# Layer 2's rows as 128 and twice 64 channels, its values kept in DRAM per pixel

## The chip, the cores and the metric

The program runs on one core of a Trainium2 chip. The core has a matrix engine (TensorE, PE in the profile), three engines for element-wise work (VectorE or DVE, ScalarE or ACT, GpSimd or POOL), a queue engine that issues most of the transfers (SyncE or SP), and 16 DMA engines. Each engine runs its own instructions in order; they wait for each other on semaphores. The metric is the device time of one execution in microseconds (us), lower is better. Three runs of the kernel before gave a median of 6404.84 us (6400.07 to 6409.53).

## The reference

Four layers follow each other on four images of 192 channels and 64 by 64 pixels in float32. The change lies in the third, "layer 2", an attention over overlapping windows of 8 by 8 pixels that stand 6 pixels apart, after three pixels of padding on each side (11 by 11 windows):

```python
DIM, HEADS, WS, OVERLAP, PAD = 192, 6, 8, 2, 3
STRIDE = WS - OVERLAP
...
y = _conv1x1(_ln_c(x, n1g, n1b), qkv_w, qkv_b)      # norm over channels, then 192 -> 576
cols = _unfold(y, WS, STRIDE, PAD)                  # zero padding comes after the projection
win = cols.reshape(B, 3 * HEADS, ch, WS * WS, L).transpose(0, 4, 1, 3, 2)
q = win[:, :, :HEADS] * temp[None, None]
k = win[:, :, HEADS:2 * HEADS]
v = win[:, :, 2 * HEADS:]
attn = jnp.einsum('blhic,blhjc->blhij', q, k) + bias[None, None]
e = jnp.exp(attn - jnp.max(attn, axis=-1, keepdims=True))
s_img = _reverse(jnp.sum(e, axis=-1, keepdims=True), H, W)      # sums folded back to pixels
o_img = _reverse(jnp.einsum('blhij,blhjc->blhic', e, v), H, W)  # outputs folded back to pixels
out = (o_img / s_img[:, :, None]).reshape(B, C, H, W)
```

What follows in layer 2 (a projection, a gate and an MLP) and the other layers (a deformable attention, a non-local block, a masked convolution) are not touched.

## The kernel before

For each image the kernel runs layer 1, then `windows()` (line 1060), the windowed attention, then the rest of layer 2 with layer 3. The image lies in DRAM (`x_flat`, of which `x_drams` is a view as two halves of 96 channels); `windows()` leaves its result in `oi` in SBUF. Constants are made early, in `constants()` (line 186), one step at a time beside the gather of the first image; there the weights of the three projections, `qkvT`, are loaded as two halves of 96 rows with a row of biases below the second, and the norm's gain, its offset and its mean are folded into them.

`windows()` goes over 11 rows of windows (`wr`). Of each row of windows only the pixel rows that are new are normed and projected; two pixel rows are shared with the row of windows before and copied by POOL (`shared`, line 1131). For one row of windows the parts are:

- `load` (1077): one transfer of the new pixel rows, 96 partitions of twice 384 pixels, into `xr`.
- `norm_steps` (1107): squares on ACT, sums over channels on PE, the inverse root on DVE and ACT, spread by PE, and two DVE products into `xs`, a padded strip of pixel rows.
- `project_rows` (1142): for each half of the channels a product for queries and one for keys, 384 columns wide, each with a first part of 96 rows (L1150) and a second of 97 (L1151, the biases included); ACT empties each into `qs` (L1154) and `ks` (L1156).
- `queries` and `inputs` (1168, 1172): POOL copies `qs` and `xs` window by window into `qw` and `xw` (L1163 to L1165).
- `scores` (1176): products of 32 rows per window and head on PE, then bias, maximum and subtraction on DVE. `exponentials` (1201): ACT, then sums on DVE.
- `turned` (1216): for each pair of windows the values are projected from `xw` (L1225) and copied by ACT (L1230); the exponentials are transposed by PE (L1233) and copied by ACT into `et` (L1237).
- `outputs` (1243): the products of values and exponentials (L1253), which fold windows into pixels in PSUM as they accumulate. `collect` (1266) copies them out, `finish` (1295) divides.

A row's 11 windows are taken in three groups of four (`g`), each group in two pairs. Products wait for a PSUM slot where they share one: the tag "a" has two slots, for the projections, the values, the transposes and the spread sums alike.

The order on each engine is written out by hand (`tc.manual_schedule()`, line 1308): what stands earlier in the loop is issued earlier on its engine. In a step of a group the next group's scores come first; then for each pair the transposes and values of this pair, the outputs of the pair before, and beside them work for later rows: in `g == 0` the projections of row `wr + 1`, one half of the channels after each pair; in `g == 1` a load and the sums of the norm of row `wr + 2`; in `g == 2` the rest of that norm, and the division for row `wr - 1`:

```python
for pair in range(WG // 2):
    ops = turned(wr, g, pair, ex)
    if due is not None:
        outputs(*due)
        ...
    due = ops
    if g == 0 and wr + 1 < NWIN:
        project_rows(wr + 1, pair)
```

SP takes its transfers in the same order. In this stage those are the loads of `xr` and, after the second row of windows, `load_image` (2022), 16 transfers of the whole image for the part that follows, with two by two partitions of 128 and 64.

Of the kernel before, what the change touches and what calls it, by code (L numbers as in the profile page):

```python
# [69 lines left out]
_WIDE = ["l0_bfc2", "l2_projb", "l2_hftw", "l2_hftb", "l2_fc2b", "l3_bias", "l3_b2"]  # L70
# [11 lines left out]
def conv_seq_kernel(ctx: ExitStack, tc: tile.TileContext, a, out: bass.AP):  # L82
# [86 lines left out]
    for i in range(3):  # L169
# [4 lines left out]
        thetaT, phiT, gT, wW, qkvT, bias, v48, headsel, fc1_dram, fc1_bias, fc1b_dram, fc1b_bias, outb,  # L174
    ) = (None for _ in range(13))
# [10 lines left out]
    def constants():  # L186

        nonlocal thetaT, phiT, gT, wW, qkvT, bias, v48, headsel, fc1_dram, fc1_bias, fc1b_dram, fc1b_bias, outb
# [13 lines left out]
        qkvT = const([P + 1, 2, 3 * C], "qkvT")  # L202
        in_turn(nc.sync.dma_start(out=qkvT[:P], in_=a["qkvT"].rearrange("(k p) n -> p k n", p=P)))
        in_turn(nc.sync.dma_start(out=qkvT[P : P + 1, 1, :], in_=a["qkvb"]))
# [56 lines left out]
        with pool_of(name="foldq", bufs=1, space=PSUM) as pp:  # L261
            p = pp.tile([128, 2, 512], F32, tag="p", name="p_qkv")
            n = 3 * C // 2
            for u in range(2):
                for k in range(2):
                    nc.tensor.matmul(
                        p[P : P + 1, u, 0:n], lhsT=V["l2_n1b"][:, k], rhs=qkvT[:P, k, bass.ts(u, n)], start=k == 0, stop=k == 1
                    )
            row = qkvT[P : P + 1, 1, :].rearrange("p (u n) -> p u n", u=2)
            nc.vector.tensor_tensor(row, row, p[P : P + 1, :, 0:n], ALU.add)  # L270
            for k in range(2):
                nc.vector.tensor_scalar_mul(qkvT[:P, k, :], qkvT[:P, k, :], V["l2_n1g"][:, k])
            centred(qkvT[:P], pp)
# [72 lines left out]
    x_flat = [dram.tile([C, HW], F32, tag=f"xd{i}", name=f"xd{i}") for i in range(2)]  # L346
    xn_drams, x_drams = ([t.rearrange("(k p) n -> p k n", p=P) for t in ts] for ts in (xn_flat, x_flat))
# [712 lines left out]
    def windows(b, oi, load_image):  # L1060
# [3 lines left out]
        with ExitStack() as s:  # L1064
# [4 lines left out]
            given, norms, xws, qws = {}, {}, {}, {}  # L1069

            def new_rows(wr):

                top = STRIDE * wr - PAD
                r0, r1 = (PAD if wr == 0 else WS - STRIDE), min(WS, H - top)
                return r0, r1, top + r0

            def load(wr, by=nc.sync):
                r0, r1, at = new_rows(wr)
                t = given[wr] = sb.tile([P, 2, 512], F32, tag="xr", name=f"xr_{b}_{wr}")[:, :, 0 : (r1 - r0) * W]
                by.dma_start(out=t, in_=x_drams[b % 2][:, :, at * W : (at + r1 - r0) * W])  # L1080
# [6 lines left out]
            for j in range(2):  # L1087
                xs = s1.tile([P + 1, 2, WS, SW], F32, tag=f"xs{j}", name=f"xs{j}_{b}")
                qs = s1.tile([P, 2, WS, SW], F32, tag=f"qs{j}", name=f"qs{j}_{b}")
                ks = s1.tile([P, 2, WS, SW], F32, tag=f"ks{j}", name=f"ks{j}_{b}")  # L1090
                for t in (xs, qs, ks):
                    nc.gpsimd.memset(t, 0.0)

                nc.gpsimd.memset(xs[P : P + 1, 1, (PAD if j == 0 else 0) : WS, inside], 1.0)
                sets.append((xs, qs, ks))
            ets = []
            for j in range(3):
                et = s1.tile([128, 3, 2, WS, WS + STRIDE], F32, tag=f"et{j}", name=f"et{j}_{b}")
                nc.gpsimd.memset(et, 0.0)
                ets.append(et)  # L1100
            rss = []
# [5 lines left out]
            def norm_steps(wr, src, dst, rows):  # L1107

                n, name = src.shape[2], f"l2n1_{b}_{wr}"
                q = n // 4  # L1110
                sq = s1.tile([P, 2, 512], F32, tag="ln_sq", name=f"sq_{name}", bufs=2)[:, :, :n]
                nc.scalar.activation(sq, src, AF.Square)
                yield SQUARE
                pv = ps.tile([128, 512], F32, tag="n", name=f"pv_{name}")
                variances(pv[:, 0:q], src, mean192)
                variances(pv[:, 128 : 128 + q], sq, mean192)
                r = s1.tile([128, 128], F32, tag="ln_r", name=f"r_{name}", bufs=2)[:, 0:q]
                spread_variance(r, pv[:, 0:q], pv[:, 128 : 128 + q])
                yield from inverse_root_steps(r, r)
                pb = spread_quarters(r, n, P, ps, name).rearrange("p (r c) -> p r c", r=rows)  # L1120
                for k in range(2):
                    nc.vector.tensor_tensor(dst[:, k], src[:, k, :].rearrange("p (r c) -> p r c", r=rows), pb, ALU.mult)

            def norm(wr, upto=None):

                r0, r1, _ = new_rows(wr)
                if wr not in norms:
                    norms[wr] = norm_steps(wr, given.pop(wr), sets[wr % 2][0][:P, :, r0:r1, inside], r1 - r0)
                links(norms[wr], upto)

            def shared(wr, i):

                to, of = sets[wr % 2][i], sets[1 - wr % 2][i]
                r1 = new_rows(wr)[1]
                if i == 0 and wr == 2:
                    nc.gpsimd.memset(to[P : P + 1, 1, PAD - 1 : PAD, inside], 1.0)
                if wr > 0:
                    nc.gpsimd.tensor_copy(to[:, :, 0 : WS - STRIDE, :], of[:, :, STRIDE:WS, :])
                if r1 < WS:
                    nc.gpsimd.memset(to[:, :, r1:WS, :], 0.0)  # L1140

            def project_rows(wr, h):

                xs, qs, ks = sets[wr % 2]
                r0, r1, _ = new_rows(wr)
# [964 lines left out]
```

## Time and profile before

| what | us |
|---|---|
| median of three runs | 6404.84 |
| the profiled execution | 6392.29 |
| its span, first to last instruction | 6390.5 |
| windows stage of the first image, from the square of its first norm at 1480.17 to the outputs' last copies at 1744 | 264 |
| pitch of two rows of windows in the middle of that stage | 23.04 |

In the stretch from 1480 to 1747 us PE is busy for 244.96 us, DVE for 160.52, ACT for 166.93 and POOL for 76.94, and the mean granted clock of PE is 0.98. The stage runs four times, once an image. The copies of finished rows (L1271) start at 1526.91, 1549.21, 1572.29, 1595.33, 1618.39, 1641.43, 1664.48, 1687.52, 1710.50, 1730.70 and 1744.02, which gives the length of each row: the first and the last ones are shorter, for they have less to do for other rows.

A line of a group reads: line of the code, engine, operation, what is written and read, then the number of instructions and their times. PE is the matrix product, PEld its loading of weights. A float32 product appears as two instructions. Where a time is followed by a bracket, that is how long the engine sat idle before, and who ended the wait.

### The profile page before, as it was taken

Reading aid. Unit: us, or ns where it says so; the run is one execution under the profiler, and the core shown is the slowest. Engines: PE = TensorE matmul, PEld = TensorE weight load, DVE = VectorE, ACT = ScalarE, POOL = GpSimd, SP = SyncE. Lnnn points to the kernel's source line nnn. Section 1 sums busy time; section 2 is a strip of 40 time slices with the busy share of each in tenths; the row PEclk is TensorE's granted clock in tenths of the full one; section 3 lists DMA queues with packets and bytes.
Section 4 is the critical chain, followed back from the end, with each engine's and each line's share of the span. In section 5 each row is a group of like instructions: output and inputs, shape, how many; then the busy total and the mean of one; then the engine's idle time right before and its main releaser. Section 6 shows DMA issues by size and latency. Waiting matters only on the chain.

```text
span 6390.5 us, 106371 instructions
## 1 busy us (share of the span) xinstructions
PE 5900.9 (92%) x40528; PEld 4039.0 (63%) x40528; DVE 4612.9 (72%) x6850; ACT 3779.2 (59%) x6552; POOL 2111.3 (33%) x2293
## 2 busy tenths in 40 slices
PE   7888999999989899999988899999998989999897
PEld 4455588886544568887654458888654457776543
DVE  3864199985677669996676839998567867765667
ACT  3764388875654358885654438887565536545542
POOL 2763077752200047772210017775220000003200
PEclk8989999999989999999999999999998999999998
DMA  6995267751010267772110057775111010001000
GB/s 193 308 316 152 81 195 223 224 178 37 24 29 17 74 200 221 226 222 69 35 36 24 21 145 227 222 223 171 36 27 29 21 57 11 13 15 38 5 7 22
DMA packets 330117, 698.60 MB, mean 109 GB/s; under 512 B 59894, under 2 KB 216838, under 8 KB 328839
## 3 DMA queue, kind: packets, MB, share of 16 engines
q0 software_dynamic: 92736, 455.22, 22.0%
q1 hardware_dynamic: 236038, 235.78, 13.5%
q8 instruction: 321, 5.26, 0.3%
q14 instruction: 190, 1.55, 0.1%
q10 hardware_dynamic: 832, 0.79, 0.0%
HBM read 611.25 MB, written 78.87 MB: 108 GB/s over the span
## 4 chain that ended last, share of the span: by engine, by line
PE 63%; DVE 20%; ACT 5%; DMA 5%; issue 4%; SPq 2%; POOL 1%; POOLq 0%; DVEq 0%; ACTq 0%
PE y L1041 11%; PE s L973 10%; PE h L650 7%; DVE ha L1403 2%; PE h L1595 2%; PE qk L1150 2%; PE v L1225 2%; PE o L878 2%; PE qk L1151 2%; DMA ring<-table,idx 2%; DVE ga L1403 2%; PE po L538 2%; DVE gate L1403 2%; DVE row L639 1%; DVE top L980 1%
## 5 line engine op out<-in xcount | busy, mean ns | idle before, releaser
L632 POOL DMA_INDIRECT ring<-table,idx x1152 | 1671.1, 1451 | 946.0 <-DVE row L639 172.7
L973 PE MATMUL s<-ths,ph 96*128 96x256 f32 x4096 | 982.5, 381 | 6.4 <-ACT sc L975 4.0
L973 PEld LDWEIGHTS s<-ths,ph 96*128 96x128 f32 x4096 | 776.6, 191 | 131.1 <-ACT sc L975 6.3
L638 ACT ACTIVATE row<-ring,pos 128x384 f32<-128x384 f32 x1152 | 673.0, 609 | 240.4 <-DVE xo L643 147.2
L639 DVE SCALAR_TENSOR_TENSOR row<-ring,fr,row 128x384 f32<-128x384 f32 x1152 | 673.1, 611 | 111.2 <-ACT row L638 106.3
L1041 PE MATMUL y<-sc,gx 128*97 128x256 f32 x3008 | 716.4, 379 | 0.0
L1041 PEld LDWEIGHTS y<-sc,gx 128*97 128x97 f32 x3008 | 489.3, 164 | 127.5 <-issue 5.1
L642 ACT ACTIVATE xo<-row,pos 128x192 f32<-128x192 f32 x1152 | 485.5, 448 | 64.2 <-PE h L650 32.2
L643 DVE SCALAR_TENSOR_TENSOR xo<-row,fr,xo 128x192 f32<-128x192 f32 x1152 | 445.4, 411 | 41.5 <-ACT xo L642 39.3
L975 ACT COPY sc<-s 128x1024 f32<-128x1024 f32 x376 | 377.1, 1003 | 157.0 <-PE s L973 154.2
L1038 DVE TENSOR_TENSOR sc<-sc,mbs 128x1024 f32<-128x1024 f32 x376 | 453.0, 1217 | 19.8 <-ACT mbs L999 19.7
L1039 ACT ACTIVATE sc<-sc 128x1024 f32<-128x1024 f32 x376 | 393.3, 1053 | 75.2 <-DVE sc L1038 72.1
L980 DVE TENSOR_TENSOR top<-top,sc 128x1024 f32<-128x1024 f32 x282 | 344.0, 1220 | 128.6 <-ACT sc L975 128.4
L650 PE MATMUL h<-ti,xo 128*128 128x192 f32 x2304 | 434.6, 327 | 0.0
L650 PEld LDWEIGHTS h<-ti,xo 128*128 128x128 f32 x2304 | 388.8, 190 | 28.8 <-issue 8.2
L1205 DVE TENSOR_REDUCE eh<-ex 128x12 f32<-128x768 f32 x132 | 125.4, 950 | 317.1 <-ACT ex L1203 317.1
L1403 DVE SCALAR_TENSOR_TENSOR ga<-gate,v,ga 128x1024 f32<-128x1024 f32 x234 | 300.3, 1283 | 6.7
L650 PE MATMUL h<-kept,xo 128*128 128x192 f32 x960 | 239.2, 381 | 70.5 <-DVE xo L643 62.0
L1645 POOL COPY gate<-gate 128x192 f32<-128x192 f32 x12 | 4.2, 348 | 904.9 <-ACT gate L1638 904.9
L650 PEld LDWEIGHTS h<-kept,xo 128*128 128x128 f32 x960 | 169.7, 210 | 162.9 <-DVE xo L643 116.4
L855 PE MATMUL h<-d_l0m,fc 128*128 128x256 f32 x768 | 217.5, 427 | 59.1 <-ACT z L1601 22.5
L1041 PE MATMUL y<-se,gx 128*97 128x256 f32 x1088 | 261.1, 380 | 0.5 <-ACT yn L1047 0.5
(402 smaller groups left out, 11090.8 us busy)
## 6 DMA issues: line engine op xcount, KB each, us to landing
ti<-table SPq DMA_DIRECT2D x768, 48.0 KB
ring<-table,idx POOLq DMA_INDIRECT x1152
xnd<-xn SPq DMA_DIRECT2D x4, 3270.0 KB
xi<-in_x_dram SPq DMA_DIRECT2D x32, 384.0 KB
xk<-xd SPq DMA_DIRECT2D x32, 384.0 KB
xd<-xc SPq DMA_DIRECT2D x64, 192.0 KB
table<-tt SPq DMA_DIRECT2D x32, 384.0 KB
xc<-xd SPq DMA_DIRECT2D x60, 192.0 KB
```

Of the source, the lines that this page charges most:

```text
L632: nc.gpsimd.indirect_dma_start(out=gt.rearrange("p q r c -> p (q r c)"), out_offset=None, in_=corners, in_offset=bass.IndirectOffsetOnAxis ...
L638: nc.scalar.activation(row, gt[:, 0], AF.Copy, scale=pos[:, t, 9 + tap : 10 + tap])
L639: nc.vector.scalar_tensor_tensor(row, gt[:, 1], fr[:, t, 9 + tap : 10 + tap], row, ALU.mult, ALU.add)
L642: nc.scalar.activation(xo[:, j, :], row[:, 0, :], AF.Copy, scale=pos[:, t, tap : tap + 1])
L643: nc.vector.scalar_tensor_tensor(xo[:, j, :], row[:, 1, :], fr[:, t, tap : tap + 1], xo[:, j, :], ALU.mult, ALU.add)
L650: nc.tensor.matmul(acc[m // 2][:, bass.ts(m % 2, C)], lhsT=xo.rearrange("p j c -> p (j c)")[:, bass.ts(m, 128)], rhs=tt, start=t == 0 and ...
L973: nc.tensor.matmul(p[:, t, :], lhsT=ph[:, bass.ts(G * g + t, 128)], rhs=ths[i], start=True, stop=True)
L980: nc.vector.tensor_tensor(tops[i], tops[i], to, ALU.max)
L1038: nc.vector.tensor_tensor(ex, ex, mbs[i].unsqueeze(1).to_broadcast([128, G, QN]), ALU.add)
L1039: nc.scalar.activation(ex, ex, AF.Exp)
L1041: nc.tensor.matmul(py, lhsT=gx[:, G * g + t, :], rhs=ex[:, t, :], start=g == 0 and t == 0, stop=g == NG - 1 and t == G - 1,)
L1403: nc.vector.scalar_tensor_tensor(acc[:, b], src(tap, b), w[:, tap : tap + 1], acc[:, b], ALU.mult, ALU.add)
```

## The change

Channels are no longer split into two halves of 96 but into 128 and 64. The upper 64 of a strip of pixel rows are kept for the left half of the strip's pixels on partitions 0 to 63 and for the right half on partitions 64 to 127, so that a strip is one tile of 128 partitions and one and a half times its pixels. A row of windows now works on the six pixel rows from `6 * wr` on (four in the last), and shares three with the row before; `qs` and `ks` are nine pixel rows high.

Queries and keys are 384 channels together: they come out as three products of 128 (`t` = 0, 1, 2: the first 128 queries, the first 128 keys, and the last 64 of both), each over the two halves of the pixels. The biases are added when ACT empties the products. Values are no longer projected once per window from copied inputs, but once per pixel (`values`), with pixels on partitions; DVE adds their bias, and they go to DRAM (`values_dram`, padded with zeros once). Sixteen transfers a row (`fetch`), one for each of the 8 pixel rows of a window and for even and odd windows, bring them back as patches, pixels of a window on partitions (`vw`). `xs`, `xw` and `inputs` are gone. In `constants()` the weights come in nine transfers in place of one and the biases in seven in place of one, and three more vectors are spread to 128 and twice 64 partitions.

```diff
-_WIDE = ["l0_bfc2", "l2_projb", "l2_hftw", "l2_hftb", "l2_fc2b", "l3_bias", "l3_b2"]
+_WIDE = ["l0_bfc2", "l2_n1g", "l2_n1b", "l2_temp", "l2_projb", "l2_hftw", "l2_hftb", "l2_fc2b", "l3_bias", "l3_b2"]
...
-        qkvT = const([P + 1, 2, 3 * C], "qkvT")
-        in_turn(nc.sync.dma_start(out=qkvT[:P], in_=a["qkvT"].rearrange("(k p) n -> p k n", p=P)))
-        in_turn(nc.sync.dma_start(out=qkvT[P : P + 1, 1, :], in_=a["qkvb"]))
+        qkvT = const([M, 2, 3 * C], "qkvT")
+        for rows, of, k in ((slice(0, M), slice(0, M), 0), (slice(0, Q), slice(M, C), 1), (slice(Q, M), slice(M, C), 1)):
...
+    values_dram = dram.tile([SW, STRIDE * (NWIN + 1), C], F32, tag="values", name="values")
...
             def load(wr, by=nc.sync):
...
+                by.dma_start(out=lo, in_=x_flat[b % 2][0:M, at : at + n])
+                for h in range(2):
+                    by.dma_start(out=hi[half(h)], in_=x_flat[b % 2][M:C, at + m * h : at + m * h + m])
...
+            if b == 0:
+                blank = s1.tile([128, 3 * C], F32, tag="blank", name="blank")
+                nc.gpsimd.memset(blank, 0.0)
+                for r in (0, 1, 2, SW - 1):
+                    nc.gpsimd.dma_start(out=values_dram[r, 0:SW], in_=blank[0:SW, 0:C])
+                inner = values_dram[PAD : PAD + H]
+                nc.gpsimd.dma_start(out=inner[:, 0:PAD, :], in_=blank[0:H].rearrange("p (w c) -> p w c", c=C))
+                nc.gpsimd.dma_start(out=inner[:, PAD + W, :], in_=blank[0:H, 0:C])
...
+            def project_rows(wr, ts):
...
+                banks = [ps2.tile([128, 512], F32, tag="a", name=f"qk_{b}_{wr}_{ts[0]}_{h}")[:, 0 : m * len(ts)] for h in range(2)]
                 for k in range(2):
+                    for j, t in enumerate(ts):
+                        for h in range(2):
+                            rows = half(h) if k else slice(0, M)
+                            nc.tensor.matmul(
+                                banks[h][:, bass.ts(j, m)], lhsT=qkvT[rows, k, bass.ts(t, M)],
+                                rhs=hi[rows] if k else lo[:, bass.ts(h, m)], start=k == 0 and j == 0, stop=k == 1,
+                                skip_group_check=True,
+                            )
...
+                        if t != 1:
+                            of = half(0) if t else slice(0, M)
+                            nc.scalar.activation(
+                                qs[of, t // 2, rows, inside], p[of], AF.Identity, bias=qkb[of, t : t + 1], scale=temp[of, t // 2]
+                            )
+                        if t == 1:
+                            nc.scalar.activation(ks[:, 0, rows, inside], p, AF.Identity, bias=qkb[:, 1:2])
+                        if t == 2:
+                            nc.scalar.activation(ks[half(0), 1, rows, inside], p[half(1)], AF.Identity, bias=qkb[half(0), 3:4])
+
+            def values(wr, part):
...
+                p = ps2.tile([128, 512], F32, tag="a", name=f"v_{b}_{wr}_{part}")[:, 0 : len(tiles) * C]
+                p = p.rearrange("p (i c) -> p i c", c=C)
+                for j, i in enumerate(tiles):
+                    for h in range(2):
+                        at = m * h + W * i
+                        nc.tensor.matmul(
+                            p[half(h), j, :], lhsT=lo[:, at : at + W], rhs=qkvT[:, 0, 2 * C :], start=j == 0, stop=False,
+                            skip_group_check=True,
+                        )
+                    for h in range(2):
+                        nc.tensor.matmul(
+                            p[half(h), j, :], lhsT=hi[half(h), bass.ts(i, W)], rhs=qkvT[half(h), 1, 2 * C :],
+                            start=False, stop=True, skip_group_check=True,
+                        )
+                nc.vector.tensor_tensor(
+                    vs[:, tiles[0] : tiles[-1] + 1, :], p, vb.unsqueeze(1).to_broadcast([128, len(tiles), C]), ALU.add
+                )
...
+                for h in range(2):
+                    r = PAD + STRIDE * wr + m // W * h
+                    nc.sync.dma_start(
+                        out=values_dram[r : r + m // W, inside, :].rearrange("r c k -> c r k"), in_=vs[half(h), 0 : m // W, :]
+                    )
+
+            def fetch(wr):
+
+                vw = vws[wr] = sb.tile([128, (NWIN + 1) // 2, C], F32, tag="vw", name=f"vw_{b}_{wr}")
+                for i in range(2):
+                    n = (NWIN + 1 - i) // 2
+                    for r in range(WS):
+                        row = values_dram[STRIDE * wr + r, STRIDE * i : STRIDE * i + 2 * STRIDE * n]
+                        at = 64 * i + WS * r
+                        nc.sync.dma_start(
+                            out=vw[at : at + WS, 0:n, :], in_=row.rearrange("(n c) k -> c n k", n=n)[0:WS]
+                        )
...
             def turned(wr, g, pair, given):
...
-                pv = ps2.tile([128, 512], F32, tag="a", name=f"v_{b}_{wr}_{g}_{pair}")[rows, 0:C]
-                for k in range(2):
-                    nc.tensor.matmul(
-                        pv, lhsT=xw[: P + k, k, both, :].rearrange("p w j -> p (w j)"), rhs=qkvT[: P + k, k, 2 * C :],
-                        start=k == 0, stop=k == 1,
-                    )
-                v = sb.tile([128, C], F32, tag="v", name=f"vs_{b}_{wr}_{g}_{pair}", bufs=3)
-                nc.scalar.copy(v[rows], pv)
...
-                rows = slice(0, 64 * len(wins))
+                rows, v = slice(0, 64 * len(wins)), vws[wr][:, wins[0] // 2, :]
...
                             if g == 0 and wr + 1 < NWIN:
-                                project_rows(wr + 1, pair)
+                                project_rows(wr + 1, ((0, 2), (1,))[pair])
+                            if g == 1 and wr + 1 < NWIN:
+                                if 2 * pair < strip(wr + 1)[1] // W:
+                                    values(wr + 1, pair)
...
                         if g == 0 and wr + 1 < NWIN:
-                            for i in (1, 2):
+                            for i in range(2):
                                 shared(wr + 1, i)
                             queries(wr + 1)
-                            inputs(wr + 1)
-                        if g == 2 and wr + 2 < NWIN:
-                            shared(wr + 2, 0)
+                        if g == 1 and wr + 1 < NWIN:
+                            fetch(wr + 1)
```

So in each row the values of the next are projected after the first and second pair of `g == 1` and stored, the fetches stand at the end of `g == 1`, and the first outputs that read them come after the second pair's transposes in `g == 0` of the next row, ahead of the second call of `project_rows`. In the first row of an image `values(0, 0)`, `values(0, 1)` and `fetch(0)` stand before the first scores.

## The prediction

> **What bounds the kernel now.** I read the page first, for the span and the chain that ended last.
>
> ```profile
> span 6390.5 us, 106371 instructions
> ...
> PE 63%; DVE 20%; ACT 5%; DMA 5%; issue 4%; SPq 2%; POOL 1%; POOLq 0%; DVEq 0%; ACTq 0%
> PE y L1041 11%; PE s L973 10%; PE h L650 7%; DVE ha L1403 2%; PE h L1595 2%; PE qk L1150 2%; PE v L1225 2%; PE o L878 2%; PE qk L1151 2%; DMA ring<-table,idx 2%; DVE ga L1403 2%; PE po L538 2%; DVE gate L1403 2%; DVE row L639 1%; DVE top L980 1%
> ```
>
> TensorE is busy in 92% of the span and carries 63% of the chain; in the second row of shares the lines of the windows stage, qk (L1150, L1151) and v (L1225), stand at some 2% each. So the change touches one stage out of several, and I went on to that stage (1480 to 1746 us in the first image) with a table of stretches. Columns: stretch, its length, then the busy time and count of PE, PE's weight loads, DVE, ACT and POOL, the granted clock, DMA share, GB/s.
>
> ```profile
> 1495.00:1500.00 5.00, 2.27 (x78) 1.78 (x75) 2.55 (x6) 0.91 (x3) 3.05 (x10) 0.81 0.03 5
> 1500.00:1503.00 3.00, 2.92 (x54) 2.29 (x53) 2.06 (x3) 1.16 (x2) 0.00 (x0) 0.50 0.29 96
> 1503.00:1506.50 3.50, 3.50 (x8) 1.78 (x7) 3.40 (x5) 1.28 (x3) 0.00 (x0) 0.50 0.00 0
> 1572.00:1595.00 23.00, 21.21 (x341) 14.02 (x341) 14.53 (x21) 15.10 (x33) 6.63 (x17) 1.00 0.05 15
> ```
>
> The last row is one row of windows in the steady state: the copies at L1271 start at 1572.29, 1595.33 and 1618.39, a pitch of 23.04. PE is busy 21.2 of 23.0 at full clock, DVE 14.5, ACT 15.1. The other rows lie in the stage's start: after a stretch in which PE worked 2.27 of 5 us the clock is 0.50, although PE is then busy all the time. The timeline of one row shows in what order the engines hold each other up (start, length, engine, line, operation; in brackets the idle time before and who ended it).
>
> ```profile
> 1624.37 0.82 PE L1151 MATMUL qk<-xs,qkvT 97*96 97x384 f32 x2
> ...
> 1625.60 0.84 ACT L1203 ACTIVATE ex<-ex 128x768 f32<-128x768 f32 x1
> 1626.47 0.95 DVE L1205 TENSOR_REDUCE eh<-ex 128x12 f32<-128x768 f32 x1 [6.16 <-ACT ex L1203]
> ...
> 1629.85 0.96 DVE L1198 TENSOR_TENSOR ex<-ex,mx 128x768 f32<-128x768 f32 x1
> ...
> 1632.03 0.92 PE L392 MATMUL pb_l2n<-r_l2n,spread 128*96 128x96 f32 x8 [1.33 <-ACT r_l2n L364]
> ...
> 1637.81 0.30 SPq L1080 DMA_DIRECT2D xr<-xd  x1
> ```
>
> In the first group of windows (g=0) PE is the bound: projections and values run back to back until the copy of ks lets ACT start the exponentials at 1625.60, and DVE had waited 6.16 for it. Then DVE is the bound: from the sum at 1626.47 to the end of the subtraction at 1630.81 it runs 4.34 without a gap, and PE waits 1.33 for the norm. SP is nearly idle: one load of a strip a row. Last, what single pieces cost (least, median and most in ns), and how long transfers keep their waiter in the chain (start, length):
>
> ```profile
> L302 SPq DMA_DIRECT2D bias<-shifted x48: 685/685/812, 177.8 to 212.2; - x48
> L1080 SPq DMA_DIRECT2D xr<-xd x36: 304/305/328, 1490.3 to 5930.5; - x36
> L1154 ACT ACTIVATE qs<-qk,v x88: 515/580/592, 1491.2 to 5985.0; 96x384 f32<-96x384 f32 x72, 96x320 f32<-96x320 f32 x16
> L1230 ACT COPY vs<-v x264: 295/318/329, 1502.6 to 6011.2; 128x192 f32<-128x192 f32 x132
> ```
>
> ```profile
> 1811.79 3.24 DMA xd<-xa
> 1815.43 2.48 DMA xa<-in_x_dram
> ...
> 1853.13 2.03 DMA xd<-xa
> ...
> 2115.40 2.96 DMA xa<-in_x_dram
> ```
>
> **Projections.** Now 16 instructions of 384 columns a row, two every 0.655 us (L1150 to L1151 at 1600.01): 5.25 us of PE. Then 24 of 192 columns; v, of that width, takes 0.65 for four, so 3.9. Twelve of these use 64 rows of the array, in pairs on opposite halves. No row of before has such a pair: if halves overlap it is 2.9, if not 3.9. The nearest row is s (L1185): 48 instructions of a third of the rows, 0.217 each, end within 0.80, so small tiles do overlap; I take 2.9, a gain of 2.3, at least 1.3.
>
> **Values.** Six pairs of windows a row cost PE six times 0.65 = 3.9 and ACT six copies of 0.318. Then three tiles, 24 instructions of 192 columns with 64 outputs each. The 64-output product at L739 ends eight of them in 0.88 where eight of 0.163 would be 1.3, so 2.0 here, 3.9 if nothing overlaps. The copies move to DVE as adds: 0.55 and 0.34 from L1299 (384 and 192 columns). They stand on DVE behind the 2.9 us of bias, maximum and subtraction, and the norm's two small operations and the next exponentials wait behind them: +0.9 on the DVE-bound part.
>
> **ACT and POOL.** Four copies of 384 columns (2.12) become eight of 192; by L1154's two sizes (580 and 515 ns for 384 and 320) one costs 0.387, together 3.1. With the value copies gone (−1.9) and a smaller square (576 for 768 columns, −0.2), ACT is some 1.1 lighter. But three projections now fill both PSUM slots of one tag at once and are emptied by six ACT instructions in a row, 2.3 us, before the next transposes get a slot: I charge PE 1.75 + 0.65 in g=0, above a bound of 0 and below 3.1. POOL loses its copies of inputs (L1163 to L1165, twice 1.16); it was waiting anyway, so nothing.
>
> **A row without its transfers.** g=0 loses 2.3 of projections and two value products (1.3) and gains 2.4 of waits: −1.2. The next part gains 0.9 on DVE and some 0.35 for a slot. The third is DVE's 5.75 with a norm product 0.14 longer, PE's savings there lying beside it. Sum 23.04 − 1.2 + 1.25 + 0.14 = 23.2; without the slot waits charged for values and half of those for projections, 22.0. I take 22.8, nearer the full charge.
>
> **The transfers.** This is the step that decides. Each row's values now go to DRAM (two stores) and return in 16 fetches of 8 partitions, each 40 or 48 pieces of 768 bytes, all on SP, which issues in order; the first fetch must wait until both stores have landed. SP also issues three loads a row for one, and 16 image loads once after the second row; these are ready early and only go ahead of it. The nearest issue is bias (L302): 8 partitions, three dimensions, back to back, 48 of them from 177.8 to 212.2, so 0.733 each. The other end is xr, 0.305, alone on its queue. I take 0.733 for shape and for standing in a row. The landings are those of the chain: a store 2.03 to 3.24, a load 2.48 to 2.96, taken as 2.5 each. So from the last add: 0.1 + 0.6 (first store) + 2.5 + 15 × 0.733 = 11.0 + 2.5 = 16.7 us. A piece costs the engines little: 13.5% of 16 engines' 6390 us over 236038 packets is 58 ns; 704 pieces a row are 2.6 us over 16 engines, 5.1 over 8, both under 11.0.
>
> The Trainium skill (DMA: Bandwidth & Descriptors, "Why a DMA increments its semaphore by 16 and not by 1") speaks against the change here: a transfer runs on as many engines as divide its outermost dimension, so 8 partitions use 8 engines, and the issuer writes the missing increments itself. No row shows the engines of bias; by the rule the data take 5.1, by a full spread 2.6, and the sum stays as issue bounds it.
>
> **Who waits.** The output product of a row's first pair stands in g=0 between the two projections and needs all 16 pieces; the second projection and all else on PE stands behind it. From that product to the last value add of the next row: product 0.45, projection and hand-over 1.05, two ACT copies and hand-over 0.9, exponentials 0.84, DVE 4.34, adds 0.9, in all 8.5. With 16.7 the ring closes at 25.2, longer than 22.8. So PE stands still about 2.4 us a row, and the savings above vanish in that wait.
>
> **Sum.** The first such product starts at 1509.66, the eleventh at 1731.82: ten pitches in 222.2. After, 252: +29.8. Start of the stage: norm done at 1490.4, projections 2.4, six copies 2.4, third projection with copies 2.0, values 2.0 + 0.6: 1499.8, and 16.7 more is 1516.5, +6.9. The last row loses 0.5. Together 36.2 an image, 145 for four. Constants: 14 more issues on SP at 101 us, some 0.5 each, and some 25 small products; PE was busy 36 of 50 us there beside the gather, which covers all but perhaps 3 (0 to 10 without cover). Zeroing the padding once is six issues of 0.68 on POOL at the stage's start, done before 1499, hidden; uncovered 4. The profiled execution took 6392.3 (span 6390.5), 12.5 under the median of 6404.84. 6392.3 + 148 = 6540, on the median's scale 6553.
>
> **Rivals.** *The fetches are hidden* (0.28): they issue at xr's 0.305 plus 0.045. The ring is 8.5 + 0.1 + 0.35 + 2.0 + 5.25 + 2.5 = 18.7, under 22.8. Then the row decides: 22.8 to 22.0 gives −2 to −10 an image, so 6362 to 6410, centre 6390: faster. For it: SP has 20 idle us a row, and simple issues are short. Against: every back-to-back row of three dimensions lies at 0.6 to 0.73. It decides below some 0.57 an issue. *The clock falls* (0.17): PE's wait follows a thin stretch, as at 1495. At half clock the product, projection, scores and values behind it double: +3 us a row of 40, 6673. For it, the 0.50 in the table after 2.27 busy of 5; against, each row also has 16 busy us. *PSUM waits alone* (0.08): fetches hidden, but the DVE adds hold slots twice as long as charged; 24.0 a row, 10 × 4 × 1.2 more than 22.8: 6435.
>
> The Trainium skill (TensorE: Matmul & The Clock Gate, "Part 1: The HAM clock gate") puts the fall at one idle window of about 3.4 us on a free-running grid. With the wait of 2.4 us and the thin work ahead of it, by the rule few rows or none would fall, 6553 to 6590; by the table's row a thin 5 us is enough in all, 6673. I side with neither alone, hence the 0.17.
>
> **How the numbers follow.** Ring as worked 0.47, hidden 0.28, clock 0.17, PSUM 0.08. The time is the ring's, 6553; its own range is 6485 (0.65 an issue) to 6606 (3.24 and 2.96 to land). To leave out no more than two in ten, the range goes into the hidden case to 6380 and the clock case to 6690. A measurement here can tell 0.2%, 12.8 us. Faster: most of hidden, 0.22; same 0.06; slower 0.72.
>
> **What would show it.** Right: the fetches on SP's queue 0.7 us apart, the first behind a wait for the stores; the copies of L1271's successor 25 us apart; PE idle before the output product with a DMA of vw named. Wrong: SP idle between rows while pitches stay at 23 or less, or issues at 0.35. A clock under 1.00 in the steady stretch speaks for the third case. If 64-row pairs do not overlap, the projections show 0.163 steps.

## The result, and the profile after

| | us |
|---|---|
| kernel before, median of four runs | 6405.28 (6400.07 to 6409.53) |
| changed kernel, median of four runs | 6599.66 (6580.27 to 6608.38) |
| ratio, with its 95% interval | 1.030 (1.0275 to 1.0324) |
| profiled execution, before and after | 6392.29 and 6608.38 |
| mean granted clock in the span, before and after | 0.963 and 0.935 |

The change costs 194 us by the medians and 216.1 between the two profiled spans. Where they lie is read from the copies of finished rows (L1271 before, L1377 after) in the two timelines. The first image's stage begins 16.3 later (1496.47 for 1480.17), and its first row is finished 10.1 later after that. The ten pitches of an image take 254.7, 251.5, 258.5 and 254.7 for 217.1, 218.9, 217.5 and 219.5: 146.4 in all. From one image's last copy to the next one's first it is 19.3, 12.5 and 13.4 more, of which 12.0, 12.7 and 10.6 lie in the first row of the image's stage, and the tail is 1.9 shorter: 16.3 + 10.1 + 146.4 + 45.2 − 1.9 = 216.1. So most of the loss is the length of a row: 23.04 before, 27.2 after (eight pitches from 1553.31 to 1771.18), and uneven, between 25.3 and 29.5.

Lines of the page after: the span, the chain's shares by engine, and the group of the transposes (count, busy time, mean ns, then its idle time and who ended most of it).

```profile
span 6606.6 us, 108025 instructions
...
PE 61%; DVE 19%; ACT 7%; DMA 5%; issue 4%; POOL 1%; SPq 1%; DVEq 0%; ACTq 0%; POOLq 0%
...
L1339 PE MATMUL t<-ident,ex 128*128 128x128 f32 x792 | 161.5, 320 | 163.3 <-ACT ks L1231 72.8
```

ACT has two more points of the chain, and what PE waits for in this stage is named as ACT's emptying of `ks`, not as a DMA. The transfers of one row in the timeline of SP, and the first output product that reads them in the timeline of PE (start, length):

```profile
1650.29 1.27 SPq L1263 DMA_DIRECT2D values<-vs  x2
1651.66 6.35 SPq L1275 DMA_DIRECT2D vw<-values  x16
```

```profile
1666.30 0.28 PE L1359 MATMUL o<-et,vw 128*32 128x88 f32 x3
```

The sixteen fetches are issued in 6.35 us, 0.40 each, all out by 1658.0. The output product that needs them starts at 1666.30, with no idle time before it. Nothing waits for them: in the whole execution an output product (L1359) waits for a fetch once, for 2.8 us. What does wait is seen in the timeline of PE and ACT a row earlier, in g = 0:

```profile
1633.03 2.58 PE L1212 MATMUL qk<-xz_l2n,qkvT 128*128 128x192 f32 x16
...
1637.44 0.55 PE L1339 MATMUL t<-ident,ex 128*128 128x128 f32 x3 [1.83 <-ACT ks L1231]
...
1639.43 1.85 PE L1212 MATMUL qk<-xz_l2n,qkvT 128*128 128x192 f32 x6 [0.41 <-ACT et L1343]
1641.20 1.18 PE L1301 MATMUL s<-ks,qw 32*64 32x64 f32 x48
...
1644.55 0.91 PE L1246 MATMUL v<-qkvT,xz_l2n 128*64 128x192 f32 x4
...
1648.84 0.55 PE L1246 MATMUL v<-qkvT,xz_l2n 128*64 128x192 f32 x4 [0.54 <-ACT et L1343]
```

```profile
1635.64 1.31 ACT L1225 ACTIVATE qs<-qk,qkb,wide 128x192 f32<-128x192 f32 x3 [1.09 <-PE qk L1212]
1636.97 0.42 ACT L1231 ACTIVATE ks<-qk,qkb 64x192 f32<-64x192 f32 x1
1637.41 0.51 ACT L1225 ACTIVATE qs<-qk,qkb,wide 64x192 f32<-64x192 f32 x1
1637.95 0.42 ACT L1231 ACTIVATE ks<-qk,qkb 64x192 f32<-64x192 f32 x1
```

Sixteen instructions (eight products) fill both slots of the tag "a"; only then does ACT begin to empty them, and the transposes get a slot 1.83 us later, behind the fourth of six emptyings. After that the same instructions are slow: four of the values take 0.91 at 1644.55 and 0.55 at 1648.84, 48 of the scores 1.18 for 0.80. The table of stretches says why (columns: stretch, length, PE, its weight loads, DVE, ACT, POOL, then the granted clock, DMA share and GB/s):

```profile
1636.00:1638.00 2.00, 0.56 (x8) 0.39 (x12) 0.83 (x1) 1.94 (x6) 1.08 (x5) 1.00 0.00 0
1638.00:1640.00 2.00, 1.59 (x20) 0.92 (x20) 0.00 (x0) 1.33 (x3) 1.03 (x3) 0.89 0.00 0
1640.00:1642.00 2.00, 2.00 (x48) 1.30 (x52) 0.00 (x0) 0.70 (x3) 0.00 (x0) 0.50 0.00 0
```

PE worked 0.56 of 2 us, and from 1639.6 on its clock is halved. Over the eight rows the clock is 0.85 after; in the steady row shown of before it was 1.00. That is a second theory beside the predicted ring of transfers: slots of PSUM that come free late, and a clock that falls behind the gaps.

### The profile page after: what moved, and what is told of

Read it like the earlier page. It is cut to its first block, busy times and chain, and to the rows that moved or that the text cites. A ratio compares the mean times of both kernels' runs of the same rounds, so it can differ in the third digit from the quotient of the medians.

```text
span 6606.6 us, 108025 instructions
## 1 busy us (share of the span) xinstructions
PE 5941.5 (90%) x40890; PEld 4037.6 (61%) x40890; DVE 4672.0 (71%) x6982; ACT 3760.1 (57%) x6466; POOL 1999.6 (30%) x1988
## 3 DMA queue, kind: packets, MB, share of 16 engines
q0 software_dynamic: 93392, 455.83, 21.3%
## 4 chain that ended last, share of the span: by engine, by line
PE 61%; DVE 19%; ACT 7%; DMA 5%; issue 4%; POOL 1%; SPq 1%; DVEq 0%; ACTq 0%; POOLq 0%
PE y L1078 11%; PE s L1010 10%; PE h L687 6%; PE qk L1212 3%; DVE ha L1511 3%; DMA ring<-table,idx 2%; PE h L1703 2%; PE po L575 2%; PE o L915 2%; DVE ga L1511 2%; PE t L1339 2%; DVE row L676 1%; DVE gate L1511 1%; DVE top L1017 1%; ACT et L1343 1%
## 5 line engine op out<-in xcount | busy, mean ns | idle before, releaser
L1075 DVE TENSOR_TENSOR sc<-sc,mbs 128x1024 f32<-128x1024 f32 x376 | 453.0, 1217 | 20.3 <-ACT mbs L1036 20.2
L1343 ACT COPY et<-t 64x384 f32<-64x384 f32 x484 | 232.0, 479 | 234.1 <-PE t L1339 228.9
L1339 PE MATMUL t<-ident,ex 128*128 128x128 f32 x792 | 161.5, 320 | 163.3 <-ACT ks L1231 72.8
L1383 POOL TENSOR_TENSOR ot<-ot,ot 102x128 f32<-102x128 f32 x80 | 36.1, 453 | 819.4 <-ACT ot L1377 754.9
```

Of the source, the lines that this page charges most:

```text
L1075: nc.vector.tensor_tensor(ex, ex, mbs[i].unsqueeze(1).to_broadcast([128, G, QN]), ALU.add)
```

## The experiments

The chips differ: the kernel before took about 6400 us on some and about 6555 on others, the difference lying mostly ahead of this stage. So ratios to the kernel before on the same chip are compared, and within a profile the pitch of a row, which does not shift with the chip.

### The ring of transfers

Stores and fetches left out (e1_no_fetch):

```diff
...
-                vw = vws[wr] = sb.tile([128, (NWIN + 1) // 2, C], F32, tag="vw", name=f"vw_{b}_{wr}")
...
+                vws[wr] = still
```

> Layer 2 neither stores the values nor fetches them as patches: the output products read one tile of zeros, so what the attention adds to the output is left out; all products, emptyings and additions stay. Ring of transfers (the prediction's likeliest case): TensorE no longer stands still for 2.4 us a row, 44 rows, so some 105 us come back: 6480 to 6510. PSUM slots and clock (the new theory, from the trace after: the last fetch lands at 1660, the product that reads it starts at 1665): nothing waits for the fetches, 6580 to 6610.

Measured 6759.54, 1.0302 (1.0269 to 1.0335) of before, against 1.030 for the change itself; its rows have the pitches of the changed kernel, 25.5, 26.9 and 29.5. The PE timeline still has the wait, and the slow products behind it:

```profile
1695.59 0.55 PE L1328 MATMUL t<-ident,ex 128*128 128x128 f32 x3 [1.89 <-ACT ks L1233]
1696.57 2.96 PE L1214 MATMUL qk<-xz_l2n,qkvT 128*128 128x192 f32 x8
1699.46 1.18 PE L1290 MATMUL s<-ks,qw 32*64 32x64 f32 x48
```

Without a single fetch the loss is the same. The ring does not set the row.

Each fetch issued twice (e4_fetch_twice):

```diff
-                        nc.sync.dma_start(
+                        for _ in range(2):
+                            nc.sync.dma_start(
```

> Each of a row's 16 fetches is issued twice, with the same data to the same place: 32 issues of 0.37 us. Ring of transfers: the row grows by 16 x 0.37 = 5.9 us, 44 rows: 6850. PSUM slots and clock: the last fetch lands at about the time at which the product needs it (some 5 us of cover, 5.9 us added): 0 to 1.5 us a row, 6595 to 6665.

Measured 7974.89, 1.216 (1.2125 to 1.2196): both numbers missed. The second fetch writes where the first does and waits until it has landed (SP waits for a transfer into `vw` 704 times, once for each second fetch), so the 32 do not take 12 us but 38, as the timeline of SP shows, and PE waits at the output product:

```profile
1622.22 38.06 SPq L1276 DMA_DIRECT2D vw<-values  x32
```

```profile
1662.21 0.37 PE L1360 MATMUL o<-et,vw 128*32 128x88 f32 x3 [27.40 <-DMA vw<-values]
```

So the ring is there, and long enough transfers do close it: a row is 54.6 us. What the prediction had wrong is how long they are.

### Slots and clock

Dummy products in the gap (e2_warm):

```diff
+                                if pair == 0:
+                                    keep_warm(ps.tile([128, 512], F32, tag="n", name=f"w_{b}_{wr}")[:, 0:384], 3)
```

> Three dummy products of 384 columns (0.65 us each at full clock) into the bank of the variances, free at that time, behind the first eight projection products of a row: they fill the 1.83 us for which TensorE waits for PSUM slots and change no wait. PSUM slots and clock: the granted clock no longer falls behind that gap; the six projections (1.85 us, at full clock 0.97), the scores (1.18, 0.80), the transposes (0.90, 0.49) and the values (2 x 0.91, 0.55) after it get back some 2.4 us a row in most of the 44 rows: 6490 to 6550, mean granted clock 0.95 or more. Slots alone, the clock without weight: 6600. Ring of transfers: 6600 or more, as the fetches set the row.

Measured 6688.01, 1.0199 (1.0164 to 1.0234): 1.0% faster than the change with more work on PE. Where no fall is left, a row takes 24.7. The timeline of PE in such a row:

```profile
1691.33 2.20 PE L790 MATMUL w<-spread,ident 128*128 128x384 f32 x6
1693.37 0.49 PE L1339 MATMUL t<-ident,ex 128*128 128x128 f32 x3
...
1698.93 0.55 PE L1246 MATMUL v<-qkvT,xz_l2n 128*64 128x192 f32 x4
```

The transposes start as late as before, but the values cost 0.55 again. From 27.2 to 24.7, 2.5 us a row, is the clock's. About every second row still had a fall, behind a thin stretch at the end of the row, so the gain, 1.0% or some 65 us, lies in the expected range but below 2.4 us in most of the 44 rows.

Filling bank by bank (e3_by_bank):

```diff
-                for k in range(2):
-                    for j, t in enumerate(ts):
-                        for h in range(2):
+                for h in range(2):
+                    for k in range(2):
+                        for j, t in enumerate(ts):
...
-                for j, t in enumerate(ts):
-                    for h in range(2):
+                for h in range(2):
+                    for j, t in enumerate(ts):
```

> The projections of a row fill one PSUM bank first and then the other, and ScalarE empties them in that order, so that its first three emptyings (1.35 us) run beside the products of the second bank; nothing else is changed. PSUM slots and clock: the transposes wait 0.3 to 0.6 us instead of 1.83, the clock stays up in most rows, 6450 to 6540. Ring of transfers: the row is as long as before, 6590 to 6610, TensorE waits for the fetches in place of the slots. If only the loss of the pairing of half-height products counts: slower by 0.1 us a row, 6605.

Measured 6664.47, 1.0174 (1.0143 to 1.0204). The steady row is 24.0, at full clock. PE's timeline shows why not less: the sixteen instructions now take 3.45 for 2.58, and the second call waits.

```profile
1721.32 3.45 PE L1212 MATMUL qk<-xz_l2n,qkvT 128*128 128x192 f32 x16
1724.70 0.55 PE L1339 MATMUL t<-ident,ex 128*128 128x128 f32 x3
1726.28 2.15 PE L1212 MATMUL qk<-xz_l2n,qkvT 128*128 128x192 f32 x8 [0.59 <-ACT ks L1231]
```

A bank of its own for the second half (e5_own_bank), on top of the last one:

```diff
-                banks = [ps2.tile([128, 512], F32, tag="a", ...)[:, 0 : m * len(ts)] for h in range(2)]
+                banks = [pool.tile([128, 512], F32, tag=tag, ...)[:, 0 : m * len(ts)] for pool, tag in ((ps2, "a"), (ps, "n"))]
...
-                p = ps2.tile([128, 512], F32, tag="a", name=f"v_{b}_{wr}_{part}")[:, 0 : len(tiles) * C]
+                p = (ps2 if part else ps).tile([128, 512], F32, tag="a" if part else "n", ...)[:, 0 : len(tiles) * C]
```

> On top of filling bank by bank (1.0174 of the kernel before, 24.0 us a row at full clock): the second bank of the projections and the first half of the values go into the bank of the variances, so that the transposes and the second half of the values find a free slot. PSUM slots and clock: the waits of 0.59 and 0.55 us and the stretched projections (3.45 us for 16 products that took 2.58) go, 22.6 to 23.3 us a row, fewer rows at half clock: 1.003 to 1.011. If slots no longer matter once the clock is up: 1.015 to 1.018. If the row has another bound close behind (VectorE's queue): 23.7 to 24.0 a row, 1.013 to 1.017.

Measured 6728.43, 1.0267 (1.0229 to 1.0305): slower than e3, although the waits for slots are gone and its undisturbed rows take 22.7. Most rows are 28.2 to 31. The table of stretches of one of them (columns as above):

```profile
1708.00:1712.00 4.00, 3.95 (x74) 2.25 (x78) 3.90 (x6) 1.49 (x4) 0.00 (x0) 1.00 0.50 107
1712.00:1716.00 4.00, 2.73 (x63) 2.18 (x48) 3.90 (x8) 3.02 (x6) 0.03 (x1) 0.86 0.39 102
1716.00:1720.00 4.00, 4.00 (x11) 2.70 (x10) 2.57 (x3) 1.71 (x4) 1.81 (x4) 0.50 0.00 0
1720.00:1724.00 4.00, 4.00 (x26) 2.55 (x26) 0.00 (x0) 2.28 (x5) 2.02 (x6) 0.50 0.02 4
1724.00:1728.00 4.00, 3.88 (x55) 2.38 (x55) 0.24 (x1) 1.57 (x3) 0.00 (x0) 0.50 0.00 0
1728.00:1732.00 4.00, 4.00 (x31) 1.73 (x30) 3.67 (x5) 2.00 (x4) 0.00 (x0) 0.51 0.00 0
```

The clock falls behind the thin end of the row (2.73 of 4 us) and stays at half for 17 us. This run parts the two causes: a kernel with shorter waits lost to one with longer waits, on the clock alone. It also gives the row without slot waits in the first two groups: 22.7. PE is busy for 19.9 us of it, for 21.2 of the 23.0 before: the products are 1.3 shorter, but PE is idle for 2.7 us instead of 1.8, mostly in waits for VectorE and ScalarE. So the 23.0 of before become 27.2 by about −0.3 for the new row without slot waits, +2.0 for slots (22.7 to 24.7; somewhat more, since bank by bank the products themselves are longer) and +2.5 for the clock.

### The order of the calls

Two calls moved (e6_order), on top of e5:

```diff
-                        if wr + 2 < NWIN and g == 2:
-                            norm(wr + 2)
...
+                            if wr + 2 < NWIN and g == 2 and pair == 0:
+                                norm(wr + 2)
+                            if g == 0 and pair == 0:
+                                early = exponentials(*nxt, sc)
...
```

> The kernel of the run with the own bank, and two calls moved: a row's first exponentials are issued ahead of its last projections (ScalarE starts them behind six emptyings instead of eight), and the scaling of the rows after next stands behind the first output scaling of a row (VectorE frees that PSUM slot 1.2 us sooner, TensorE waits no 0.90 us for the inverse root). PSUM slots and clock: 0.5 to 1.5 us a row less than with the own bank alone, ratio lower by 0.004 to 0.010. If TensorE's own work sets the row by then: within 0.002.

Measured 6564.68, 1.0023 (1.0000 to 1.0045), more than expected; rows of 21.5 us, of about 23 where the clock falls once. The loads of the constants given to another queue, and the three new vectors widened later (e7_constants):

```diff
-            in_turn(nc.sync.dma_start(out=to[:, 2 * C :], in_=src[:, 2 * C :]))
+            in_turn(nc.scalar.dma_start(out=to[:, 2 * C :], in_=src[:, 2 * C :]))
...
```

> The kernel of the run with the moved calls; the 16 loads of the projection's constants are issued by ScalarE's queue, which stands idle then, and the three new vectors are widened in a product of their own behind the folding of the two larger matrices. If the 16 us ahead of the first image's stage come from SP's longer chain of issues and the longer product ahead of the gather: 10 to 16 us less than with the moved calls, ratio lower by 0.0015 to 0.0025. If they come from something else: no change within 4 us.

Measured 6571.34, 1.0030 (1.0010 to 1.0050): no gain, and the first stage begins at 1599.53 for 1597.90; with the old layout on the same chip (e8, below) it begins at 1581.17. The 16 us ahead of the stage are not explained by those issues. In the timeline of e6's row one wait is left, for the exponentials, which stand on ACT behind the norm's inverse root:

```profile
1718.41 0.55 PE L1339 MATMUL t<-ident,ex 128*128 128x128 f32 x3 [1.63 <-ACT ex L1319]
```

Exponentials ahead of it (e9_exp_first), on top of e6:

```diff
-                        if wr + 2 < NWIN and g == 1:
-                            norm(wr + 2, INVERSE)
                         if g == 0:
                             ex = early
                         elif nxt[0] < NWIN:
                             ex = exponentials(*nxt, sc)
+                        if wr + 2 < NWIN and g == 1:
+                            norm(wr + 2, INVERSE)
```

> The kernel of the run with the moved calls (1.0023; rows of 21.5 us, and of 23 where the clock falls), and in the second group of a row the exponentials are issued ahead of the inverse root of the rows after next: ScalarE starts them about 2.9 us sooner, so that TensorE no longer waits 1.63 us for them; that wait is most of the 3.4 us in which TensorE works 0.52 of the time, after which the clock falls. PSUM slots and clock: rows of 20.0 to 21.2 us and hardly one with a fall, 0.990 to 0.997. Clock without weight: 21.0 us a row at best, 0.998 to 1.001. Ring of transfers, measured at 0.37 us an issue: 16 x 0.37 + 0.6 + 2.5 + 2.5 + 8.5 = 20.0 us a row, below which no row can come.

Measured 6355.24, 0.9928 (0.9913 to 0.9943), rows of 19.8, below the 20.0 that the ring was said to allow. And five dummy products at each stage's start (e10_warm_start):

```diff
+                keep_warm(ps.tile([128, 512], F32, tag="n", name=f"warm1_{b}")[:, 0:384], 2)
...
+                        if wr == 0 and g == 0:
+                            keep_warm(ps.tile([128, 512], F32, tag="n", name=f"warm3_{b}")[:, 0:384], 3)
```

> The same, and five dummy products at the start of each image's stage, two behind the first scores and three behind the second, into the bank of the variances, where TensorE waits 1.55 and 2.06 us; today the clock falls there for 17 us in the first image. Clock: the first row of an image's stage gets back 3 to 8 us, four images 12 to 32 us, ratio lower than without them by 0.002 to 0.005. Clock without weight: no change within 0.001.

Measured 6319.52, 0.988 (0.9863 to 0.9898): the fastest of all, ahead of both kernels. The first image's first row ends 49.8 us into its stage for 57.0. In this kernel the ring begins to show: in the whole execution an output product waits for a fetch seven times, 10.2 us in all. The longest row is the third pitch of the first image, in which SP has the twelve and more loads of the next part ahead of the fetches. Timelines of SP and PE, and the stretches:

```profile
1583.00 6.41 SPq L1275 DMA_DIRECT2D vw<-values  x16
```

```profile
1591.31 0.28 PE L1359 MATMUL o<-et,vw 128*32 128x88 f32 x3 [1.29 <-DMA vw<-values]
```

```profile
1590.00:1594.00 4.00, 2.71 (x22) 1.73 (x22) 1.14 (x2) 2.93 (x7) 2.02 (x6) 0.72 0.33 88
1594.00:1598.00 4.00, 4.00 (x69) 2.67 (x70) 1.25 (x2) 0.97 (x3) 0.00 (x0) 0.50 0.00 0
```

A wait of 1.29 us for a fetch, then half clock: this row takes 24.0 for 19.8. The second image has one of 23.8, the third none, the fourth two of about 21.

### Controls

The fastest version without fetches (e12_no_fetch_warm, the edit of e1 on e10):

> The fastest version (0.988, rows of 19.8 us and a few of 24) without storing the values and fetching them, the output products reading a tile of zeros; what the attention adds to the output is left out. Ring of transfers at the measured issue time (20.0 us a row by the prediction's sum): now it binds, rows of 18.5 to 19.5, 0.975 to 0.985. Transfers still hidden: 19.8 a row, within 0.002 of the version with them.

Measured 6453.69, 0.9855 (0.9837 to 0.9873); the intervals overlap. Its rows are 19.8, all of them from the second pitch to the seventh, those of 24.0 are gone. So the transfers stay hidden even at 19.8, but for one or two rows in three of the four images. What sets the row now is PE: with or without fetches it is busy for 19.7 of the 19.8 us.

The moved calls in the kernel before: first the two of e6 (e8_before_order), then all, with the dummy products (e11_before_all). Their edits are those of e6, e9 and e10.

> The kernel before with the same two calls moved and nothing else: what of the moved calls' gain belongs to the order alone. If TensorE at full clock sets its row of 23.0 us: within 0.2% of the kernel before. If waits for VectorE and ScalarE are a part of its row too: 0.5 to 1.5 us a row, 0.985 to 0.996.

> The kernel before with the same moved calls (both exponentials, the scaling) and the same five dummy products at the start of an image's stage, without the change: what order alone brings the old layout. If the old row of 23.0 us is TensorE's own work and its waits were small: 22.3 to 23.1 a row, 0.994 to 1.002, so that the changed layout in the same order (0.988) is ahead by what its products save. If the order is all: 19.8 us a row as in the changed kernel, 0.985 to 0.990.

Measured 6577.84, 1.0025 (0.9996 to 1.0055), and 6549.76, 1.0007 (0.9989 to 1.0025): nothing, with rows of 23.1 (24.7 where the clock falls) and 22.8. In the row of 22.8 PE is busy for 21.3 us, and one wait is left, for the copy of the values on ACT, which holds a slot of the tag "a":

```profile
1719.50 0.89 PE L1298 MATMUL rb<-rs,headsel 128*96 128x384 f32 x2 [1.56 <-ACT vs L1230]
```

In the new layout, in the same order, the row is 19.8. Of the 3 us between the two rows about 1.5 are shorter products (21.3 to 19.7 busy) and 1.5 this wait, which the new layout does not have, for its values no longer pass through ACT. Whether the old layout would lose it too with a bank of its own there was not tried. So the layout, in an order that suits it, saves 3 us a row; as it was put in, slots and clock took that and 4 more.

## Why the prediction was near and its reason wrong

The time forecast, 6553, lies 47 below the measured one, and the range held it. The likeliest case did not happen, so the nearness of the number is luck.

- **The step that failed** is the price of a fetch: "I take 0.733 for shape and for standing in a row." The queue shows 0.302 us at the median and 0.40 from one to the next, by the end that was set aside (xr's 0.305). The row that was taken, bias, has the same 8 partitions, but copies 2 KB from SBUF to SBUF where a fetch brings 30 or 36 KB from DRAM; why its issue takes longer is not shown. With it the prediction's own ring is 0.1 + 0.6 + 2.5 + 15 × 0.40 + 2.5 + 8.5 = 20.2, far under 27.2; e1 shows that nothing waits, e4 that the ring exists, and the rows of 19.8 that in the moved order it is shorter still. The knee it gave, 0.57 an issue, stands between the two prices.
- **The rival "fetches are hidden"** was right about the transfers and wrong about the time: it let the row be 22.8, and the row was 27.2.
- **The row without its transfers** was priced 22.8 with 2.4 us of slot waits; at full clock it measured 24.7 (e2). The waits in g = 0 were 1.83 and 0.41 for the 1.75 and 0.65 charged, that before the values 0.54 for 0.35: well priced. The products, which a row at 22.8 has shorter, were not: the projections take 2.58 for sixteen instructions and, at full clock in e2, 0.59 and 1.12 for eight, 4.3 instead of 2.9; the values 2.85 (six fours at 0.475) instead of 2.0. The 64-row halves do overlap, as was taken (last section): the eight such instructions take 0.92 of the 2.58, where eight at 0.163 would be 1.3. What the sum left out are pauses: in the weight loads of these sixteen there is one of 0.19 for the second slot, and one of 0.23 before the change from 128 rows to 64. An emptying costs 0.42 to 0.51 for the 0.387 taken.
- **The rival "the clock falls"** had the right end of the chain with the wrong trigger. It was to follow the wait for a fetch; it followed the waits for slots and the thin end of the row. Its price, 3 us a row, measured 2.5.
- **"PSUM waits alone"**, 24.0 a row, is close to the 24.7 of full clock; its reason, slots held longer by DVE's adds, was not: ACT's six emptyings held them.
- **Small terms.** DVE's adds: 0.56 and 0.36 for 0.55 and 0.34. The stage's start to its first output product: 34.5 after 29.5, +5.0 for +6.9 predicted; to its first finished row +10.1, and +12.0, +12.7 and +10.6 in the other images. Constants: +16.3 for 3, above the bound of 10. In the trace the gather begins 4.6 later and PE waits 6.40 for a weight that SP issues later, for 3.10 before; as e7 brought nothing, what makes up the rest is open.
- **Two sums.** The row without the slot waits for values (0.35) and half of those for projections (1.2) is 23.2 − 1.55 = 21.7, not 22.0. And the 6485 for 0.65 an issue is on the scale of the profiled execution; on the median's, on which 6553 and 6606 stand, it is 6498. Neither decides anything.

## What to carry to other kernels

The row of the same queue that looked nearest to the new transfers gave the wrong price: 0.733 where 0.40 was measured. Where two prices lie on two sides of a knee, keep both, let the knee and not a likeness of shapes say how sure the sum can be, and read the time from one issue to the next from the first trace that has such transfers. When a product is split so that several banks are filled at once and then emptied in a row by one engine, ask what stands next on TensorE and which slot it needs, and give the second bank a place of its own; here that took the waits away at once, but paid only when the clock held as well. A gap of 2 us on TensorE costs more than 2 us if the clock falls behind it: look at the granted clock before pricing a faster row, and compare rows at equal clock.

## What the runs showed of the hardware

The falls of the clock lie on a fixed grid. In the changed kernel, read from stretches of 0.2 us, they come at 1578.13, 1584.96, 1612.26, 1639.57, 1660.05, 1666.88 and 1694.18: 6.83, 27.30, 27.31, 20.48, 6.83 and 27.30 apart, which is 2, 8, 8, 6, 2 and 8 times 3.413 us. The Trainium skill (TensorE: Matmul & The Clock Gate, "Part 1: The HAM clock gate") has a free-running window of 3.413 us, and the trace agrees. It lets the clock fall after an idle window; here no window was idle. In the changed kernel and nine of the runs built on it (all but e4), 155 falls lie between the first and the ninth finished row of an image. They followed grid windows in which PE was busy for 0.39 to 0.68 by the trace; windows of 0.52 to 0.66 were also passed without a fall, and none above 0.68 was followed by one. (In the last two rows of an image single falls followed windows of up to 0.77.) So the trace's busy share is not exactly what is counted, and what is, stays open.

That a row of 24.0 us, 7.03 windows, kept its clock (e3) and one of 22.7, 6.65 windows, did not (e5) fits such a grid: the thin stretch meets another part of the window in each row. This is argued, not shown.

The same sixteen instructions took 2.58 us with the two 64-row halves in turn and 3.45 with one half after the other. The weight loads in the two timelines, of the changed kernel and of e3 (start, length, count at the end):

```profile
1634.69 0.63 PEld L1212 LDWEIGHTS qk<-xz_l2n,qkvT 64*128 64x128 f32 x8 [0.23 <-issue]
```

```profile
1722.16 0.62 PEld L1212 LDWEIGHTS qk<-xz_l2n,qkvT 64*128 64x128 f32 x4 [0.23 <-issue]
1723.01 0.62 PEld L1212 LDWEIGHTS qk<-xz_l2n,qkvT 128*128 128x128 f32 x4 [0.22 <-ACT ot L1378]
```

Eight loads on alternating halves take as long as four on one half, so the two halves run beside each other; and before each change of rows the loads stand idle for 0.22 to 0.23 us, once in the first order, three times in the second. The Trainium skill (TensorE: Matmul & The Clock Gate, "Part 3: Packing small matmuls — row/col tiling") says that a load of weights runs beside products only on other rows of the array. This trace does not bear out the "only": in e3 sixteen loads (0.62 for four, 2.5 in all) and sixteen products (2.6 at 0.163) are done in 3.45, though each load but those at a change is for the rows that the product ahead of it uses.
